# A key mask moved from TensorE products into the distances of an attention, and another order of loads in the feed-forward after it

## The chip, the cores and the metric

The kernel runs on one core of a Trainium2 chip. The metric is the time of one execution on the device in microseconds (us); the median of three runs stands for a kernel. A core has TensorE (PE: matrix products and transposes; PEld is its loading of weights, which overlaps the products), VectorE (DVE), ScalarE (ACT), GpSimd (POOL) and SyncE (SP). Each engine takes its instructions in the order in which they were written down for it and stops at one whose inputs or buffers are not ready. SyncE does no arithmetic: its queue issues nearly all transfers between the large memory (HBM) and the on-chip memory (SBUF). Products land in PSUM, from where VectorE or ScalarE must fetch them.

## The reference

Two transformer blocks run one after the other on an input of 4 batches x 1024 rows x 512 columns; each has 16 heads of 32 columns and a feed-forward of width 2048. Only the first block is touched by the change. Cut to what matters:

```
h = layer_norm(x) * (1 + scale) + shift           # scale, shift from the condition
q, k, v = split(h @ Wqkv)
scores = q @ k.T / sqrt(32) - torus_dist * torus_scale[head]
scores = where(mask[key], scores, -1e30)
x = x + softmax(scores) @ v @ Wout
x = x + gelu(layer_norm(x) @ W1 + b1) @ W2 + b2
```

`torus_dist` is one matrix of 1024 x 1024 for all batches and heads, `mask` has one bit for each batch and key, and `torus_scale` one number for each head. In the inputs of these runs every mask bit is set. The second block has an attention without mask or distances, and quantised linear layers.

## The kernel before

**Stages.** The kernel runs in four stages: first attention (to about 1590 us), first feed-forward (to about 2475), second attention (to about 3740), second feed-forward.

**The first attention** is worked off in units. A unit is a batch b, a group hg of four heads, and a tile of 128 query rows; the loops run over 4 batches, 4 head groups and 8 query tiles, 128 units in all. For each unit and each head j there is a tile `e` of 128 x 1024 values (queries x keys):

1. `begin` (L679 to L691) has GpSimd scale the distances of the query tile by the head's `torus_scale` into `e` (L689). At the first head it issues the load of that query tile's distances (L686); there are two buffers (`dp`).
2. `scores` (L258) makes, for one half c of the keys at a time, the four heads' scores (L267; the query is scaled by minus one over the root of 32, so that signs are reversed). Then, where there is a mask, four more products (L274), each of one row of ones with one row of the mask, add 1e30 at masked keys in the same PSUM bank. `masked` (L587) makes that row for a batch: it loads the bytes of the mask and GpSimd turns them into bf16 (L596).
3. `half_l0` (L694) lets VectorE add scores and `e`, write the sum back to `e`, and keep the row's running minimum (L696).
4. `weigh` lets ScalarE take the exponential (L450).
5. `turn` transposes the weights on TensorE, four blocks at a time (L291), and ScalarE or VectorE copies them to tiles `pt` (L294), whose tags pt0 and pt1 hold the two halves of the keys.
6. `product` multiplies them with v (L303), once for two units.

**Order.** All engines' orders are written out by hand: in the loop at the end of `attention` unit i makes its scores while unit i-1 is transposed and unit i-3's pair is multiplied. After each half, two `begin` calls of unit i+1 follow. Into eight slots of each unit a plan puts pieces of other work: the next head group's q, k and v (L648, L666), the last batch's output projection (`project`: loads of x at L471, products at L722, a VectorE add at L728, a store at L729), the statistics and transposed input of the next batch, and `sums`, which prepares combinations of W1 and W2 for the feed-forward and stores them as w1s and w2s. SyncE's queue holds all their transfers in the same written order.

**Buffers.** `e` tiles come from a pool of 9 (`sp`), `pt` tiles from 6 for each tag.

**The first feed-forward** works on 8 blocks of 512 rows, with seven products in place of eight at either layer (the numbered combinations 1 to 7 of quarters). `first(f)` does the first layer for one of eight pieces f of the width (L1060); its weights come with `load_w1` (L1006), one ring of two for numbers 1, 2, 6, 7, 5 (tile w1e, L1009) and one for 3, 4 (w1l, L1011). `second(n)` does the second layer for number n in the order 1, 2, 6, 7, 5, 3, 4 (L1121) and issues the loads of the next number's weights (w2q, L1025) ahead, from W2 itself or from w2s. Each `second` has two steps, 14 in a block; at some of them work for the next block is done: `rows` loads its four input tiles (L961, 1 MB), `normed` normalises them, four `turned` transpose them, `summed` makes the input's combinations. Every second step advances `beside`, which quantises the second block's weights piece by piece: `ternary` loads a piece (tile wpiece, L192, a pool `stage` of 2), reduces or scales it on VectorE and converts it on GpSimd. At its end `quantised_input` prepares the second attention's first input through tiles `xn`.

Of the kernel before, what the change touches and what calls it, by code (L numbers as in the profile page):

```python
# [30 lines left out]
F32 = mybir.dt.float32  # L31
BF16 = mybir.dt.bfloat16
U8 = mybir.dt.uint8
# [20 lines left out]
FMAX = 3.0e38  # L54
BIG = 1e30

MAGIC = 12582912.0
# [10 lines left out]

Order = namedtuple("Order", "evict exps block back even odd")
ORDER_L0 = Order(("AAAA", "AAAD"), ((1, 2), (1, 2)), 2, (1, 2), (1, 2, 3, 5, 6, 7), (3, 6))  # L70
ORDER_L1 = Order(("AADA", "AAAD"), ((1, 2), (2, 2)), 0, (0, 2), (2, 6, 7), (2, 3, 6, 7))


@with_exitstack
def two_blocks(ctx: ExitStack, tc: tile.TileContext, a: dict, out: bass.AP):
# [18 lines left out]
    nc.gpsimd.memset(ones, 1.0)  # L94
    onesb = const.tile([P, P], BF16, name="onesb")
    nc.gpsimd.memset(onesb, 1.0)
    eps_ln = const.tile([P, 1], F32, name="eps_ln")
# [85 lines left out]
    def ternary(stage, small, psum, mean, src, dst):  # L183
# [6 lines left out]
        def load(view):  # L190
            w = stage.tile([P, 2 * D], F32, name="wpiece")[:, :size]
            nc.sync.dma_start(w.rearrange("p (m n) -> p m n", m=shape[1]), view)  # L192
            return w
# [33 lines left out]

    def attention(pools, parts, softmax, clean, masked, pieces, early, guarded, order, aside, last):


# [19 lines left out]
        stats, prep, qkv, project = parts  # L250
        heads, sums, pt, es, lows, o_tiles, mask, accs = {}, {}, {}, {}, {}, {}, {}, {}

# [3 lines left out]
        def scores(u, c):  # L256
            b, hg, qc, qi = u
            qt = qc * NQ + qi  # L258
            if c == 0:
                if qi == 0:  # L260
                    sums[b, hg, qc] = small.tile([P, NQ, HPG], F32, name="sums")
                lows[u] = small.tile([P, HPG, 2], F32, name="low")
            qT, kT, _ = heads[b, hg]
            s = [ps_s.tile([P, 512], F32, name="scores", tag="s") for _ in range(HPG)]
            for j in range(HPG):
                rows = slice(j * HD, (j + 1) * HD)
                nc.tensor.matmul(  # L267
                    s[j], lhsT=qT[rows, bass.ts(qt, P)], rhs=kT[rows, bass.ts(c, 512)],
                    start=True, stop=mask[b] is None,
                )  # L270
            if mask[b] is not None:
                for j in range(HPG):
                    row1 = slice(j * HD, j * HD + 1)
                    nc.tensor.matmul(  # L274
                        s[j], lhsT=onesb[row1, :], rhs=mask[b][row1, bass.ts(c, 512)],
                        start=False, stop=True,
                    )
            for j in range(HPG):
                half(es[u, j], lows[u][:, j, :], c, s[j])
# [4 lines left out]
        def turn(u, j, h2, engine):  # L284

            b, hg, qc, qi = u
            if qi == 0:
                pt[b, hg, qc, j, h2] = pts.tile([P, LT // 2, QC], F32, name="pt", tag=f"pt{h2}")
            tr = ps_mm.tile([P, LT // 2, P], F32, name="tr", tag="mm")
            for k in range(LT // 2):  # L290
                nc.tensor.transpose(  # L291
                    tr[:, k, :], es[u, j][:, bass.ts(h2 * (LT // 2) + k, P)], ident
                )
            engine(pt[b, hg, qc, j, h2][:, :, bass.ts(qi, P)], tr)  # L294
# [106 lines left out]
        for s, n in enumerate(late):  # L401
            plan.setdefault(s, []).insert(0, (begun, n))
        mask[0] = masked(0)
        for j in range(HPG):
            start(units[0], j)
        ready = None
        with tc.manual_schedule(engines=ALL):
            for i in range(end + (3 if last else nu)):
# [3 lines left out]
                for c in range(2):  # L412
# [28 lines left out]
                    if i + 1 < end:  # L441
                        after = units[i + 1]
                        if c == 0 and after[0] not in mask:
                            mask[after[0]] = masked(after[0])
                        for j in (0, 1) if c == 0 else (2, 3):
                            start(after, j)
# [16 lines left out]
    with ExitStack() as st:  # L463
# [13 lines left out]
        dp = st.enter_context(tc.tile_pool(name="l0d", bufs=2))  # L477
        sp = st.enter_context(tc.tile_pool(name="l0s", bufs=9))
        small = st.enter_context(tc.tile_pool(name="l0small", bufs=4))
# [107 lines left out]

        def masked(b):

            if b == 0:  # L590
                m8 = m0
            else:
                m8 = tmp.tile([P, L], U8, name="m8", bufs=1)
                nc.sync.dma_start(m8, a["mask"][b].partition_broadcast(P))
            m = tmp.tile([P, L], BF16, name="maskb")
            nc.gpsimd.tensor_scalar(m, m8, -BIG, BIG, ALU.mult, ALU.add)  # L596
            return m

# [78 lines left out]

        dists, ahead = {}, [dist0]

        def begin(b, hg, qt, j):  # L680
            if j == 0:
                if ahead:
                    dists[qt] = ahead.pop()
                else:
                    dists[qt] = dp.tile([P, L], F32, name="dist")
                    nc.sync.dma_start(dists[qt], a["L0_cond_torus_dist"][0, bass.ts(qt, P), :])  # L686
            h = hg * HPG + j
            e = sp.tile([P, L], F32, name="e")
            nc.gpsimd.tensor_scalar(  # L689
                e, dists[qt], tscale[:, h : h + 1], 1.0, ALU.mult, ALU.mult  # L690
            )  # L691
            return e

# [39 lines left out]
        def sums():  # L733
# [44 lines left out]
            (small, pts, tmp, op, ps_s, ps_mm, ps_acc), (stats, prep, qkv, project),  # L778
            (begin, half_l0, exponentials), clean, masked,
            (LT + 1, LT + 2 * KT + 4, 24, 1 + 3 * LT, 12, [2] * 6), early=False, guarded=True,  # L780
# [14 lines left out]

    def modulate(pool, x, rstd, rows):
        xn = pool.tile([P, D], F32, name="xn")
        nc.vector.scalar_tensor_tensor(xn, x, rstd, rows[:, 0, :], ALU.mult, ALU.mult)  # L798
        nc.gpsimd.tensor_tensor(xn, xn, rows[:, 1, :], ALU.add)  # L799
        return xn  # L800
# [23 lines left out]
    def quantised_input(n, b, source, scale, pools, engine):  # L824


        adap, xp, tmp, small, psum, home = pools
        rows = ada_load(adap, n, b)
# [3 lines left out]
        for t in range(LT + 4):  # L832
            if t < LT:
                at = b * LT + t
                x = xp.tile([P, D], F32, name="xr")
                nc.sync.dma_start(x, source[at])
                xns[t] = modulate(tmp, x, scale[:, at : at + 1], rows)
            if 0 <= t - 2 < LT:
# [22 lines left out]
    with ExitStack() as st:  # L861
# [8 lines left out]
        tmp = st.enter_context(tc.tile_pool(name="f0t", bufs=3))  # L870
        stage = st.enter_context(tc.tile_pool(name="f0st", bufs=2))
        adap = st.enter_context(tc.tile_pool(name="f0ada", bufs=1))
# [41 lines left out]
        def beside():  # L914
# [22 lines left out]
            for n in (1, 2):  # L937
# [16 lines left out]
            yield from quantised_input(  # L954
                1, 0, x2, rms2, (adap, xin, tmp, small, ps_mm, w1p), nc.vector
            )
# [49 lines left out]
        def load_w1(f):  # L1006

            e = w1ring.tile([P, 5, 2, P], F32, name="w1e")
            nc.sync.dma_start(e, w1s[:, f, :5])  # L1009
            late = w1ring.tile([P, 2, 2, P], F32, name="w1l")  # L1010
            nc.sync.dma_start(late, w1s[:, f, 5:])  # L1011
            return {
                1: e[:, 0], 2: e[:, 1], 6: e[:, 2], 7: e[:, 3], 5: e[:, 4], 3: late[:, 0],
                4: late[:, 1],
            }

# [157 lines left out]
        with tc.manual_schedule(engines=ALL):  # L1174
            done = None
            for blk in range(nblk):
# [3 lines left out]
                if blk + 1 < nblk:  # L1180
# [14 lines left out]

                    steps[1], steps[4], steps[11] = [rows], [normed], [summed]
                    for k in range(KT):
                        steps[7 + k] = [lambda k=k: turned(k)]
                block(now["x"], now["t"], steps, blk + 1 < nblk)
# [66 lines left out]
    with ExitStack() as inner:  # L1266
# [12 lines left out]
        def first_of_ffn():  # L1279

            row_scale3(0, B - 1)
            pools = adap, xp, utmp, small, ps_mm, w1p
            yield from quantised_input(2, 0, x3, rms3, pools, nc.gpsimd)
# [4 lines left out]
        def prep(b):  # L1288
            home = hp if b % 2 else w1p
            pools = adap, xp, utmp, small, ps_mm, home  # L1290
            return quantised_input(1, b, x2, rms2, pools, nc.gpsimd) if b else iter(())
# [40 lines left out]
        def half_l1(e, low, c, s):  # L1332
# [6 lines left out]
            (small, pts, utmp, op, ps_s, ps_mm, ps_acc), (stats, prep, qkv, project),  # L1339
            (begin, half_l1, exponentials), nc.scalar.copy, lambda b: None,  # L1340
            (0, LT + 4, 12, LT + 4, 8, [1] * 4), early=True, guarded=False, order=ORDER_L1, aside=None,
# [9 lines left out]
    with ExitStack() as inner:  # L1351
# [16 lines left out]
        def normed(t):  # L1368
            xs[t] = xfp.tile([P, D], F32, name="xr")
            nc.sync.dma_start(xs[t], x3[t])  # L1370
            if t < LT:
                xqTs[t] = xqT[2, 0][:, :, bass.ts(t, P)], deqs[2, 0][:, t : t + 1]
                return
            if t % LT == 0:
                rows[t // LT] = ada_load(adap, 2, t // LT)
            xns[t] = modulate(fp, xs[t], rms3[:, t : t + 1], rows[t // LT])

# [152 lines left out]
```

## Time and profile before

| | us |
|---|---|
| median of three runs (4037.19 to 4039.2) | 4037.45 |
| the profiled execution | 4035.59 |
| its span in the profile | 4033.8 |
| first attention, 31 to 1590 | 1559 |
| first feed-forward, 1590 to 2475 | 885 |

How to read the profile: a row of a group names the line of the kernel, the engine, the operation, its output and inputs by the program's names, their shapes and the number of instructions; behind the bar stand the busy time in us and the mean length of one in ns; behind the second bar the idle time of the engine just before these instructions, and what ended it. The lengths of successive products overlap[...]; distances between starts show their price better. In a list in order of time a line holds start and length in us, and in brackets how long the engine had stood idle and what released it. The chain of waits goes from the last instruction back through whatever released each one; its shares say which lines set the end. DMA share is the mean busy share of the core's 16 DMA engines.

### The profile page before, as it was taken

What the parts mean: (1) busy time and instruction counts of PE and PEld (TensorE: products, weight loads), DVE (VectorE), ACT (ScalarE), POOL (GpSimd) and SP (SyncE); (2) the same over time, 40 slices, a digit from 0 to 9 for tenths busy, and PEclk for the clock granted to TensorE, in tenths of its full rate; (3) what the DMA queues carried; (4) which work ended last, traced back from release to release, by engine and by line L of the source; (5) the groups of instructions that cost most, each with busy time, mean ns of one, the idle gap of its engine ahead of it and who ended that gap; (6) DMA issues with size and microseconds to landing.
All of it is one profiled execution on the core that took longest, in us unless ns stands there. A gap on an engine that the chain in (4) does not pass through costs nothing.

```text
span 4033.8 us, 80643 instructions
## 1 busy us (share of the span) xinstructions
PE 3912.5 (97%) x30352; PEld 2591.5 (64%) x30403; DVE 2669.2 (66%) x6706; ACT 2557.4 (63%) x4666; POOL 1357.1 (34%) x1468
## 2 busy tenths in 40 slices
PE   8999999999999999999999999999999999999999
PEld 5666556655665565788878886666566566565554
DVE  5666565656664556555555644788788888778798
ACT  5777667766776677222222223888888788888676
POOL 3444344434443442343344430020120211202677
PEclk9999999999999999999999999999999999999999
DMA  4222222222222212666677542000100100101321
GB/s 146 69 77 78 67 89 73 81 74 89 73 80 75 78 59 93 193 221 213 210 243 230 188 150 89 1 28 4 40 27 2 43 17 12 43 2 35 136 74 45
DMA packets 198909, 357.68 MB, mean 89 GB/s; under 512 B 19108, under 2 KB 86220, under 8 KB 198392
## 3 DMA queue, kind: packets, MB, share of 16 engines
q1 hardware_dynamic: 197256, 348.77, 27.2%
q8 instruction: 240, 3.93, 0.4%
q10 hardware_dynamic: 1264, 3.75, 0.3%
q14 instruction: 149, 1.22, 0.1%
HBM read 303.13 MB, written 49.32 MB: 87 GB/s over the span
## 4 chain that ended last, share of the span: by engine, by line
PE 85%; ACT 7%; DVE 3%; DMA 2%; issue 1%; POOL 0%; SPq 0%; POOLq 0%; ACTq 0%; DVEq 0%
PE tr L291 21%; PE scores L267 13%; PE acc L303 12%; PE qk_ps L648 5%; ACT e L450 4%; PE v_ps L666 3%; PE out_ps L722 3%; ACT pt L294 3%; PE pw L1060 3%; PE pz L1060 3%; PE py L1060 3%; PE px L1121 3%; PE h_ps L1409 2%; PE o_ps L1448 2%; PE py L1121 2%; PE pw L1121 2%
## 5 line engine op out<-in xcount | busy, mean ns | idle before, releaser
L294 ACT COPY pt<-tr 128x512 f32<-128x512 f32 x1664 | 908.6, 593 | 572.6 <-PE tr L291 568.5
L291 PEld LDWEIGHTS tr<-ident,e 128*128 128x128 f32 x8192 | 897.9, 141 | 526.7 <-issue 256.9
L450 ACT ACTIVATE e<-e,low 128x1024 f32<-128x1024 f32 x1024 | 1183.8, 1164 | 2.7 <-DVE e L1333 2.0
L291 PE MATMUL tr<-ident,e 128*128 128x128 f32 x8192 | 1129.7, 279 | 35.7 <-ACT e L450 18.4
L689 POOL TENSOR_SCALAR e<-dist,tscale 128x1024 f32<-128x1024 f32 x512 | 572.2, 1121 | 910.8 <-PE tr L291 812.2
L696 DVE CUSTOM_DVE_ANT_0 e<-scores,e,low 128x512 f32<-128x512 f32 x512 | 353.9, 747 | 340.9 <-PE scores L274 340.9
L303 PE MATMUL acc<-pt,v 128*32 128x256 f32 x8192 | 498.4, 384 | 0.0
L303 PEld LDWEIGHTS acc<-pt,v 128*32 128x32 f32 x8192 | 241.4, 110 | 250.8 <-issue 119.9
L696 DVE CUSTOM_DVE_ANT_0 e<-scores,e 128x512 f32<-128x512 f32 x512 | 323.1, 687 | 113.4 <-PE scores L274 113.4
L1333 DVE TENSOR_SCALAR_CACHE_REDUCE e<-scores,low 128x512 f32<-128x512 f32 x512 | 353.6, 747 | 66.9 <-PE scores L267 66.1
L294 DVE COPY pt<-tr 128x512 f32<-128x512 f32 x384 | 264.1, 688 | 195.9 <-PE tr L291 195.9
L1333 DVE TENSOR_SCALAR_CACHE_REDUCE e<-scores 128x512 f32<-128x512 f32 x512 | 322.8, 686 | 28.8 <-PE scores L267 27.8
L267 PE MATMUL scores<-qkT 32*128 32x512 f32 x2048 | 329.3, 640 | 2.4 <-ACT qkT L1324 1.4
L267 PE MATMUL scores<-kT,qT 32*128 32x512 f32 x2048 | 317.1, 640 | 0.8 <-DVE kT L661 0.8
L1315 POOL COPY v<-qk 128x128 f32<-128x128 f32 x128 | 40.1, 314 | 661.4 <-DVE qk L1312 510.7
L648 PE MATMUL qk_ps<-hT,wqkv 128*128 128x512 f32 x512 | 255.2, 595 | 0.0
L450 ACT ACTIVATION_READ_ACCUMULATOR e<-e,low 128x1 f32 x1024 | 210.8, 206 | 0.0
L1066 ACT ACTIVATE a<-y,vcols 128x256 f32<-128x256 f32 x128 | 65.1, 508 | 196.9 <-DVE y L1082 104.5
L1074 ACT COPY s<-px 128x256 f32<-128x256 f32 x64 | 22.8, 356 | 236.0 <-PE px L1060 197.0
L267 PEld LDWEIGHTS scores<-kT,qT 32*128 32x128 f32 x2048 | 95.6, 183 | 97.7 <-issue 59.6
L799 POOL TENSOR_TENSOR xn<-xn,ada 128x512 f32<-128x512 f32 x64 | 81.5, 1274 | 193.0 <-DVE xn L798 193.0
L267 PEld LDWEIGHTS scores<-qkT 32*128 32x128 f32 x2048 | 100.4, 183 | 69.1 <-issue 31.6
(229 smaller groups left out, 5626.7 us busy)
## 6 DMA issues: line engine op xcount, KB each, us to landing
dist<-n_L_cond_torus_dist_dram SPq DMA_DIRECT2D x128, 512.0 KB
w1e<-w1s SPq DMA_DIRECT2D x64, 640.0 KB
xr<-x SPq DMA_DIRECT2D x136, 256.0 KB
w2q<-w2s SPq DMA_DIRECT2D x128, 256.0 KB
w2q<-in_L_cond_W_dram SPq DMA_DIRECT2D x96, 256.0 KB
x_in<-in_x_dram SPq DMA_DIRECT2D x84, 256.0 KB
w1l<-w1s SPq DMA_DIRECT2D x64, 256.0 KB
x<-xr SPq DMA_DIRECT2D x64, 256.0 KB
```

Source lines behind the costliest of these rows:

```text
L267: nc.tensor.matmul(s[j], lhsT=qT[rows, bass.ts(qt, P)], rhs=kT[rows, bass.ts(c, 512)], start=True, stop=mask[b] is None,)
L291: nc.tensor.transpose(tr[:, k, :], es[u, j][:, bass.ts(h2 * (LT // 2) + k, P)], ident)
L294: engine(pt[b, hg, qc, j, h2][:, :, bass.ts(qi, P)], tr)
L303: nc.tensor.matmul(acc[j * HD : (j + 1) * HD, :], lhsT=v[:, k, j * HD : (j + 1) * HD], rhs=pt[b, hg, qc, j, k // (LT // 2)][:, k % (LT // ...
L450: nc.scalar.activation(e, e, AF.Exp, bias=low, scale=-1.0, accum_out=total)
L648: nc.tensor.matmul(mm, lhsT=wqkv[:, k, bass.ds(n * D + hg * P, P)], rhs=hT[b][:, k, bass.ts(half, 512)], start=(k == 0), stop=(k == KT - 1),)
L666: nc.tensor.matmul(mm[:, i, :], lhsT=hT[b][:, k, bass.ts(half * 4 + i, P)], rhs=wqkv[:, k, bass.ds(2 * D + hg * P, P)], start=(k == 0), st ...
L689: nc.gpsimd.tensor_scalar(e, dists[qt], tscale[:, h : h + 1], 1.0, ALU.mult, ALU.mult)
L696: nc.vector.tensor_tensor_reduce(out=e, in0=s, in1=e, op0=ALU.add, op1=ALU.min, scale=1.0, scalar=low[:, 0:1] if c else 3.0e38, accum_out= ...
L1060: nc.tensor.matmul(o, lhsT=w[n][:, k, :], rhs=moving[n][:, k, :], start=k == 0, stop=k == 1)
L1121: nc.tensor.matmul(p[:, t], lhsT=hid[f][n][:, bass.ts(t, P)], rhs=w[f // 2][:, f % 2], start=f == 0, stop=f == FH - 1,)
L1333: nc.vector.tensor_scalar(e[:, bass.ts(c, 512)], s, -SCALE, low[:, 0:1] if c else 3.0e38, ALU.mult, ALU.min, accum_out=low[:, c : c + 1],)
```

## The change

The mask products and `masked` are gone, and with them the row of ones. In their place the distances are marked: for each batch GpSimd makes the 16-bit pattern of a bf16 NaN at masked keys and zero elsewhere (`make_bar`), and VectorE adds it to each of the batch's eight distance tiles (`bar`), which are stored in HBM (`barred`) while they are used for the first head group. Head groups 1 to 3 load the stored tiles. GpSimd's scaling now takes the minimum with 1e30 as its second operation, where it multiplied by 1 before; [...]masked keys get 1e30.

The load of a distance tile is now issued one unit earlier in the written order, in the first `begin` of the unit before; the next batch's mask is loaded at the last head group's first tile and converted at its fourth. The `bar` of a tile stands behind the last `begin` of the unit before it. The pool of `e` has 10 buffers, pt0 of the first attention 5.

In the first feed-forward w1 is loaded in three tiles (numbers 1, 2; then 6, 7, 5; then 3, 4); the pieces of `ternary` have three buffers, which `quantised_input` shares for its `xn`; and `rows`, `normed`, `turned` and `summed` stand one step later. The core of the diff:

```diff
-ORDER_L0 = Order(("AAAA", "AAAD"), ((1, 2), (1, 2)), 2, (1, 2), (1, 2, 3, 5, 6, 7), (3, 6))
+ORDER_L0 = Order(("AAAA", "AAAD"), ((1, 2), (1, 2)), 2, (1, 2), (1, 2, 3, 5, 6, 7), (3, 6), (5, 6), ((0, 1), (2, 3)))
...
-                    start=True, stop=mask[b] is None,
+                    start=True, stop=True,
                 )
-            if mask[b] is not None:
-                for j in range(HPG):
-                    row1 = slice(j * HD, j * HD + 1)
-                    nc.tensor.matmul(
-                        s[j], lhsT=onesb[row1, :], rhs=mask[b][row1, bass.ts(c, 512)],
-                        start=False, stop=True,
-                    )
...
-                pt[b, hg, qc, j, h2] = pts.tile([P, LT // 2, QC], F32, name="pt", tag=f"pt{h2}")
+                pt[b, hg, qc, j, h2] = pts.tile([P, LT // 2, QC], F32, name="pt", tag=f"pt{h2}", bufs=order.pts[h2])
...
-        sp = st.enter_context(tc.tile_pool(name="l0s", bufs=9))
+        sp = st.enter_context(tc.tile_pool(name="l0s", bufs=10))
...
+        def load_mask(b):
+            m8s[b] = tmp.tile([P, L], U8, name="m8", bufs=1)
+            nc.sync.dma_start(m8s[b], a["mask"][b].partition_broadcast(P))
+
+        def make_bar(b):
+            bits = tmp.tile([P, L], mybir.dt.uint16, name="bar", bufs=1)
+            nc.gpsimd.tensor_scalar(bits, m8s.pop(b), -QNAN, QNAN, ALU.mult, ALU.add)
+            bars[b] = bits[:, :].bitcast(BF16)
+
+        def load_dist(b, hg, qt):
+            d = dists[b, hg, qt] = dp.tile([P, L], F32, name="dist")
+            nc.sync.dma_start(
+                d, barred[b][qt] if hg else a["L0_cond_torus_dist"][0, bass.ts(qt, P), :]
+            )
+
+        def bar(b, qt):
+            d = dists[b, 0, qt]
+            nc.vector.tensor_tensor(d, d, bars[b], ALU.add)
+            nc.sync.dma_start(barred[b][qt], d)
+
+        make_bar(0)
+        bar(0, 0)
...
         def begin(b, hg, qt, j):
-            if j == 0:
-                if ahead:
-                    dists[qt] = ahead.pop()
-                else:
-                    dists[qt] = dp.tile([P, L], F32, name="dist")
-                    nc.sync.dma_start(dists[qt], a["L0_cond_torus_dist"][0, bass.ts(qt, P), :])
+            n = (b * NHG + hg) * LT + qt + 1
+            after = n // (NHG * LT), n // LT % NHG, n % LT
+            if after[0] == B:
+                after = None
...
-                e, dists[qt], tscale[:, h : h + 1], 1.0, ALU.mult, ALU.mult
+                e, dists[b, hg, qt], tscale[:, h : h + 1], BIG, ALU.mult, ALU.min
             )
+            if j == 0 and after:
+                load_dist(*after)
+                if hg == NHG - 1 and b + 1 < B and qt == 0:
+                    load_mask(b + 1)
+            if j == HPG - 1:
+                dists.pop((b, hg, qt))
+                if hg == NHG - 1 and b + 1 < B and qt == 3:
+                    make_bar(b + 1)
+                if after and after[1] == 0:
+                    bar(after[0], after[2])
             return e
...
-        stage = st.enter_context(tc.tile_pool(name="f0st", bufs=2))
+        stage = st.enter_context(tc.tile_pool(name="f0st", bufs=3))
...
-            e = w1ring.tile([P, 5, 2, P], F32, name="w1e")
-            nc.sync.dma_start(e, w1s[:, f, :5])
-            late = w1ring.tile([P, 2, 2, P], F32, name="w1l")
-            nc.sync.dma_start(late, w1s[:, f, 5:])
+            w = {}
+            for at, numbers in ((0, (1, 2)), (2, (6, 7, 5)), (5, (3, 4))):
+                n = len(numbers)
+                t = w1ring.tile([P, n, 2, P], F32, name=f"w1_{at}")
+                nc.sync.dma_start(t, w1s[:, f, at : at + n])
+                w |= {number: t[:, i] for i, number in enumerate(numbers)}
+            return w
...
-                    steps[1], steps[4], steps[11] = [rows], [normed], [summed]
+                    steps[2], steps[5], steps[12] = [rows], [normed], [summed]
                     for k in range(KT):
-                        steps[7 + k] = [lambda k=k: turned(k)]
+                        steps[8 + k] = [lambda k=k: turned(k)]
```

## The prediction

> **What bounds the kernel now.** I read the totals first, then the stages, the chain of waits of the first attention, the groups, and short stretches in order of time. The totals, and busy time by stage (span, PE, PEld, DVE, ACT, POOL; then TensorE clock, DMA share, GB/s):
>
> ```profile
> PE 3912.5 (97%) x30352; PEld 2591.5 (64%) x30403; DVE 2669.2 (66%) x6706; ACT 2557.4 (63%) x4666; POOL 1357.1 (34%) x1468
> ```
> ```profile
> 31.00:1590.00 1559.00, 1545.81 (x13199) 944.82 (x13198) 912.43 (x2630) 1120.28 (x2031) 627.43 (x639) 1.00 0.24 74
> 1590.00:2475.00 885.00, 854.47 (x3995) 722.69 (x3994) 466.05 (x763) 178.64 (x370) 325.04 (x378) 0.99 0.64 205
> ```
>
> The first attention (31 to 1590 us) keeps TensorE busy 99% of its time, with ScalarE at 72%, VectorE at 59%, GpSimd at 40% and the DMA engines at 24%. The first feed-forward (1590 to 2475) has TensorE at 97% and DMA at 64%. Only these two stages are touched. The chain of waits of the first 1600 us, by line, and the groups of the touched instructions:
>
> ```profile
> by line: PE tr L291 30.0%; PE scores L267 17.3%; PE acc L303 14.7%; PE qk_ps L648 13.2%; PE v_ps L666 7.0%; PE out_ps L722 5.5%; PE scores L274 3.8%; ACT e L450 1.8%; ACT pt L294 1.6%; PE acc L325 0.8%; PE tr_x L456 0.7%; issue 0.6%; PE tr_
> ```
> ```profile
> L689 POOL TENSOR_SCALAR e<-dist,tscale 128x1024 f32<-128x1024 f32 x512 | 572.2, 1121 | 910.8 <-PE tr L291 812.2 <-ACT e L450 29.6 <-issue 28.4
> ...
> L696 DVE CUSTOM_DVE_ANT_0 e<-scores,e 128x512 f32<-128x512 f32 x512 | 323.1, 687 | 113.4 <-PE scores L274 113.4
> ...
> L1121 PE MATMUL py<-w2q,a 128*128 128x256 f32 x512 | 124.3, 395 | 20.7 <-DMA w2q<-w2s 11.5 <-DMA w2q<-in_L_cond_W_dram 9.1
> ...
> L274 PE MATMUL scores<-maskb,onesb 1*128 1x512 bf16 x1024 | 120.1, 376 | 0.0
> ```
>
> The mask products (L274) stand on the chain with 3.8% of 1600 us, 61 us; ScalarE's two lines together have 3.4%. VectorE waits for L274, never the other way round for long. GpSimd's scalings wait for free buffers, not the reverse.
>
> **Part 1, the mask products go.** There are 1024, in 256 groups of four (128 units, two halves). Their busy time of 120.1 us overlaps with neighbours, so I take distances between starts. A half of the first attention, and one of the second attention, which has no mask:
>
> ```profile
> 717.73 1.14 PE L267 MATMUL scores<-kT,qT 32*128 32x512 f32 x8
> 718.69 0.40 PE L274 MATMUL scores<-maskb,onesb 1*128 1x512 bf16 x4
> 719.02 1.09 PE L291 MATMUL tr<-ident,e 128*128 128x128 f32 x8
> ```
> ```profile
> 2707.08 1.14 PE L267 MATMUL scores<-qkT 32*128 32x512 f32 x8
> 2708.15 0.66 PE L291 MATMUL tr<-ident,e 128*128 128x128 f32 x4
> ```
>
> With masks, scores to the next transpose is 1.29 us; the masks themselves take 719.02 - 718.69 = 0.33 us. Counted so, the saving is 256 x 0.33 = 84 us. But the Trainium skill, TensorEngine Tiling (Array Packing), Key Properties, says that a change of tiling mode drains TensorE: scores and masks both use 32-row tiles, the transposes the full array, so the drain before the transposes stays. The second attention agrees: without masks the same distance is 1.07 us, so a group is worth 1.29 - 1.07 = 0.22 us: **256 x 0.22 = 56 us**. I take that; the chain's 61 us (0.24 each) is the upper end. Lower end: half, 28 us, if ScalarE sets the pace in the short units. Why I don't expect that: in a bare pair of units (7.6 + 10.9 = 18.5 us from score start to score start, at 404) ScalarE has 8 exponentials at 1.14 and 14 copies at 0.47, 15.7 us, still under 18.5 - 0.86 = 17.6.
>
> **Part 2, GpSimd's scaling with a minimum.** No row has a minimum on GpSimd. Nearest is the same instruction with two multiplies, 1121 ns; a multiply and an add on 2048 elements (L1427) takes 1972, the same 0.83 ns per further element, so the second operation's kind does not show. I take 1.12 us again: nothing. Upper end: the price of its two-input add (L799, 1274 ns per 512, so 2.5 us): 10.0 us per unit, over the bare pairs alone (20.0 against 17.6): 19 such pairs, up to +46 us. No gain is possible, as GpSimd isn't on the chain.
>
> **Part 3, the barred distances.** New: 32 VectorE adds of 128x1024, 32 stores and no more loads than now (128); four conversions of a mask, as now (L596, 1.04 us). VectorE takes 424 ns for 256 columns (L1082) and 692 for 512 (L1086), so I estimate 1.23 us for 1024; 32 x 1.23 = 39 us of an engine that is 41% idle. They stand at the end of a unit, before the evictions of the next, where VectorE looks like this (a bare unit):
>
> ```profile
> 403.83 0.69 DVE L294 COPY pt<-tr 128x512 f32<-128x512 f32 x1 [1.22 <-PE tr L291]
> 405.14 0.69 DVE L696 CUSTOM_DVE_ANT_0 e<-scores,e 128x512 f32<-128x512 f32 x1 [0.62 <-PE scores L274]
> ```
>
> Free time there is 0.62 us (0.3 less once the masks are gone), so an add delays the four evictions by about 0.9 us. That reaches TensorE only where the second scores follow 3 us later and wait for a bank; the units of a first head group measure 7.6, 10.9, 16.2, 14.8, 19.0, 14.0, 24.3, 15.6 us in batches 1 to 3. So one or two adds per batch are on the path: about 4 x 0.9, **+4 us**. Ends: 0, and all 32 exposed, +39.
>
> A rule speaks against this part. SBUF — State Buffer, Who interferes with whom: a VectorE instruction with two SBUF inputs and a GpSimd one that reads SBUF block each other; whichever starts first holds the pair to its end. The trace agrees:
>
> ```profile
> 1724.91 0.68 DVE L998 TENSOR_TENSOR t<-hT,hT 128x512 f32<-128x512 f32 x1
> 1725.08 1.20 POOL L222 TENSOR_SCALAR wq<-wpiece 128x768 bf16<-128x768 f32 x1 [2.56 <-DVE wpiece L216]
> 1725.63 1.19 DVE L999 TENSOR_TENSOR hT<-hT 128x512 f32<-128x512 f32 x1
> ```
>
> The GpSimd op takes 1.20 in place of 0.83, the second add 1.19 in place of 0.69. By the rule every add could wait out one scaling, 32 x 1.12 = +36 us more. I don't charge it: the scalings of the unit after next wait for this very add, and those of the next unit end in the middle of the current one, so GpSimd is mostly idle at that moment.
>
> DMA: 32 stores of 512 KB, 16.8 MB. At 24% busy they are hidden; without that cover, at the 306 GB/s of the first 31 us, 1.7 us each, 55 us. SyncE's queue: a store waits for its add at the end of a unit; behind it stand the loads of x (L471), the stores of x1 (L729), the quarters (L744) and the next distance (L686). The next distance has at least half a unit to land (4 us or more); x loads in that part already wait for L728 and the store before them (134.5 us in SyncE's waits), so they lose little. At the start the first add runs behind the normalisation that ends at 25.5, and GpSimd's four scalings then end near 32, before the first eviction at 33.28: 0.
>
> One pt buffer less (5 of the first half's tiles) is neutral: when the fifth is needed for the second transposed pair, the four products that free the oldest have just run ahead of it on TensorE. The tenth e buffer lets GpSimd run a quarter of a unit earlier, which nobody waits for: 0.
>
> **Part 4, the first feed-forward.** TensorE idles 20.7 us for w2q (row L1121 above) and 3.0 us for w1e (row L1060 px). One case:
>
> ```profile
> 1810.21 0.33 SPq L192 DMA_DIRECT2D wpiece<-in_L_cond_w_ada_dram  x1
> 1810.64 0.38 SPq L1025 DMA_DIRECT2D w2q<-w2s  x1
> ...
> 1814.44 1.13 PE L1121 MATMUL py<-w2q,a 128*128 128x256 f32 x4 [1.16 <-DMA w2q<-w2s]
> ```
>
> SyncE stands at L192 until a weight piece is released by work that VectorE does behind the normalisation; the w2 load behind it lands late. A third piece buffer lets L192 pass one step earlier: of the 11.5 us I take 8. The other 9.1 are loads issued late, then in company of 1 MB of x1 (L961); that megabyte moves one step later: 3 gained, but it now stands ahead of half the loads for the third product: 7 blocks x 0.5 = 3.5 lost. w1 in three loads (64 more issues, 0.4 us each on SyncE, which has room) starts the needed 256 KB alone: 2 gained. The input sums end near 1731 in place of 1728, before TensorE's 1733 to 1735: 0. Sum **-9 us**; ends -24 (all idle time) and +15 (7 blocks with a stall of about 2).
>
> **Sum** against the profiled execution (4035.6 us, span 4033.8 and 1.8 around it): 4035.6 - 56 + 4 - 9 = 3974.6. The median of the runs shown stands 1.9 above it, so **3977** (3976.5 rounded up).
>
> **Rivals.** (a) ScalarE takes over as the bound: for it speaks that ScalarE is already at 72% of a stage that gets shorter, with 54 us (3.4%) on the chain; against it the 15.7 of 17.6 above. Masks 28: 4035.6 - 28 + 4 - 9 + 1.9 = 4004. (b) The feed-forward's new order of loads collides at 205 GB/s: -56 + 4 + 15 gives 4001. (c) Slower: the add waits on VectorE for its own distance, whose load was issued only half a unit before (256 KB issued at 1810.64 served TensorE at 1814.44, 3.8 us); in-order VectorE holds the evictions, TensorE the banks. At 3 us each, 32 x 3 = 96: 4035.6 - 56 - 9 + 96 + 1.9 = 4068. It decides from (56 + 9)/32 = 2.0 us each on the path; against it, the units there are mostly 14 to 24 us long. (d) No change, if mask products were hidden: their 61 us on the chain says no.
>
> **How the numbers follow.** Likeliest 0.66, (a) 0.15, (b) 0.12, (c) 0.05, (d) 0.02. About 0.2% (8 us) can be told from no change. Low end: -61 - 24 and bars free: 4035.6 - 85 + 1.9 = 3952. High end 4006 takes in (a) and (b). Faster 0.92 (a little of (a) and (b) falls short), same 0.03, slower 0.05.
>
> **What would show it.** No L274; scores to transposes 1.07 us; the scaling still 1.12; 32 adds near 1.23 with little of TensorE's wait behind them; bare pairs near 17.6; L1121's idle under 12; the stages near 1508 and 876 us. Wrong if the scaling exceeds 2 us, if VectorE waits for distances, or if ScalarE's lines grow past 80 us on the chain.

## The result

The changed kernel takes 4486.2 us (median of 4, 4480.3 to 4489.1) against 4037.3 us before (median of 4): 1.111 times the time, 95% interval 1.109 to 1.113. The forecast was 3977 us, faster. Totals and the first attention's stretch of the changed kernel (it now ends near 2045 us; columns as before: span, PE, PEld, DVE, ACT, POOL, then TensorE clock, DMA share, GB/s), and the chain of waits up to there:

```profile
PE 4152.2 (93%) x29379; PEld 2684.9 (60%) x29379; DVE 2729.0 (61%) x6738; ACT 2565.9 (57%) x4666; POOL 2687.4 (60%) x1467
```
```profile
31.00:2045.00 2014.00, 1782.74 (x12097) 1036.06 (x12096) 973.07 (x2650) 1120.13 (x2014) 1956.41 (x642) 0.89 0.20 65
```
```profile
by line: POOL e L696 27.7%; PE tr L284 18.5%; PE scores L267 12.5%; PE acc L296 9.8%; PE qk_ps L658 7.3%; issue 6.4%; PE out_ps L739 3.4%; PE v_ps L676 3.2%; DVE e L713 2.5%; ACT e L440 2.2%; ACT pt L287 1.6%; DMA x_in<-in_x_dram 0.7%; PE a
```

GpSimd was busy for 40% of this stage and is now busy for 1956 of 2014 us. It stands first on a chain on which it did not stand at all. The groups of the touched instructions say why:

```profile
L696 POOL TENSOR_SCALAR e<-dist,tscale 128x1024 f32<-128x1024 f32 x512 | 1900.1, 3711 | 48.1 <-DVE mv L520 1.6
L713 DVE CUSTOM_DVE_ANT_0 e<-scores,e 128x512 f32<-128x512 f32 x512 | 339.7, 689 | 587.5 <-POOL e L696 508.3
L267 PE MATMUL scores<-kT,qT 32*128 32x512 f32 x2048 | 485.4, 674 | 210.5 <-DVE low L713 209.6
...
L603 DVE TENSOR_TENSOR dist<-dist,bar 128x1024 f32<-128x1024 f32 x32 | 42.8, 1339 | 5.0 <-DMA dist<-n_L_cond_torus_dist_dram 5.0
L1138 PE MATMUL py<-w2q,a 128*128 128x256 f32 x512 | 117.3, 381 | 9.4 <-DMA w2q<-w2s 6.0 <-DMA w2q<-in_L_cond_W_dram 3.3
```

One scaling with the minimum takes 3.71 us, where one with two multiplies took 1.12. Four make 14.8 us per unit, more than a unit lasted (12.2 us on average). VectorE waits 508 us for them and holds the score banks, and TensorE, which idled 0.8 us before its scores in the kernel before, idles 210 us behind it. Most of the rest of the longer stage counts as busy TensorE time: scores that start two at a time as banks fall free (485 us busy for 317), and work at a lower clock (0.89 for 1.00). The last two rows are those of the prediction's other steps: 32 adds of 1.3 us whose own waits come to 5 us, and a wait for w2q that fell in this row from 20.7 to 9.4 us (in all rows of the line from 20.8 to 12.4).

### The profile page after: what moved, and what is told of

Read it like the earlier page. It is cut to its first block, busy times and chain, and to the rows that moved or that the text cites. A ratio compares the mean times of both kernels' runs of the same rounds, so it can differ in the third digit from the quotient of the medians.

```text
span 4478.5 us, 78517 instructions
## 1 busy us (share of the span) xinstructions
PE 4152.2 (93%) x29379; PEld 2684.9 (60%) x29379; DVE 2729.0 (61%) x6738; ACT 2565.9 (57%) x4666; POOL 2687.4 (60%) x1467
## 3 DMA queue, kind: packets, MB, share of 16 engines
q14 instruction: 149, 1.22, 0.1%
## 4 chain that ended last, share of the span: by engine, by line
PE 70%; POOL 13%; ACT 7%; DVE 4%; issue 4%; DMA 2%; SPq 0%; POOLq 0%; ACTq 0%; DVEq 0%
PE tr L284 17%; POOL e L696 13%; PE scores L267 11%; PE acc L296 10%; ACT e L440 4%; PE qk_ps L658 3%; ACT pt L287 3%; PE pw L1077 2%; PE pz L1077 2%; PE py L1077 2%; PE px L1138 2%; PE h_ps L1426 2%; PE out_ps L739 2%; PE o_ps L1465 2%; PE py L1138 2%
## 5 line engine op out<-in xcount | busy, mean ns | idle before, releaser
L696 POOL TENSOR_SCALAR e<-dist,tscale 128x1024 f32<-128x1024 f32 x512 | 1900.1, 3711 | 48.1 <-DVE mv L520 1.6
L284 PEld LDWEIGHTS tr<-ident,e 128*128 128x128 f32 x8192 | 958.3, 148 | 600.9 <-issue 325.5
L284 PE MATMUL tr<-ident,e 128*128 128x128 f32 x8192 | 1198.0, 291 | 33.7 <-ACT e L440 16.2
L713 DVE CUSTOM_DVE_ANT_0 e<-scores,e 128x512 f32<-128x512 f32 x512 | 339.7, 689 | 587.5 <-POOL e L696 508.3
L267 PE MATMUL scores<-kT,qT 32*128 32x512 f32 x2048 | 485.4, 674 | 210.5 <-DVE low L713 209.6
L296 PE MATMUL acc<-pt,v 128*32 128x256 f32 x8192 | 536.4, 406 | 0.2 <-DVE o L322 0.2
L296 PEld LDWEIGHTS acc<-pt,v 128*32 128x32 f32 x8192 | 252.4, 116 | 278.4 <-issue 159.5
L267 PEld LDWEIGHTS scores<-kT,qT 32*128 32x128 f32 x2048 | 131.6, 191 | 405.5 <-DVE low L713 325.6
L658 PE MATMUL qk_ps<-hT,wqkv 128*128 128x512 f32 x512 | 265.8, 617 | 0.0
L1110 POOL TENSOR_TENSOR a<-z,a 128x256 f32<-128x256 f32 x64 | 47.5, 741 | 279.4 <-ACT z L1083 279.4
```

The lines of the kernel that those rows point to most:

```text
L267: nc.tensor.matmul(s[j], lhsT=qT[rows, bass.ts(qt, P)], rhs=kT[rows, bass.ts(c, 512)], start=True, stop=True,)
L284: nc.tensor.transpose(tr[:, k, :], es[u, j][:, bass.ts(h2 * (LT // 2) + k, P)], ident)
L296: nc.tensor.matmul(acc[j * HD : (j + 1) * HD, :], lhsT=v[:, k, j * HD : (j + 1) * HD], rhs=pt[b, hg, qc, j, k // (LT // 2)][:, k % (LT // ...
L658: nc.tensor.matmul(mm, lhsT=wqkv[:, k, bass.ds(n * D + hg * P, P)], rhs=hT[b][:, k, bass.ts(half, 512)], start=(k == 0), stop=(k == KT - 1),)
L696: nc.gpsimd.tensor_scalar(e, dists[b, hg, qt], tscale[:, h : h + 1], BIG, ALU.mult, ALU.min)
L713: nc.vector.tensor_tensor_reduce(out=e, in0=s, in1=e, op0=ALU.add, op1=ALU.min, scale=1.0, scalar=low[:, 0:1] if c else 3.0e38, accum_out= ...
```

## The experiments

Where the stages stand in the runs, from the first starts of their products in each trace: the first attention's scores from first to last, and from the feed-forward's first product to the second attention's first scores. These two columns are of one execution each; two executions of the same version (multiply by one) gave 1497.5 and 1493.6 us of scores, and the four runs with the old feed-forward 838.8 to 847.9 us for it. Each ratio is to runs of the kernel before on the same chip.

| | scores, us | feed-forward, us | median of the runs, us | to before (95%) |
|---|---|---|---|---|
| before | 1547.0 | 843.0 | 4037.3 | |
| changed | 2013.6 | 821.9 | 4486.2 | 1.111 (1.109 to 1.113) |
| multiply by one | 1497.5 | 824.1 | 3969.6 | 0.983 (0.982 to 0.985) |
| the same, old feed-forward | 1496.6 | 838.8 | 3980.9 | 0.986 (0.985 to 0.987) |
| before, new feed-forward | 1546.9 | 828.3 | 4026.5 | 0.998 (0.997 to 0.999) |
| before, no mask products | 1491.3 | 847.9 | 3982.2 | 0.987 (0.985 to 0.988) |
| before, with the minimum | 2021.1 | 839.6 | 4509.8 (one run) | |

**The minimum taken back.** The first run keeps the whole change but for that one operation. So that masked keys still come out, 1e30 is added to their distances in place of a NaN (right for positive scales, which these inputs have). No key is masked in these inputs, so no run shows either mark at work, nor what GpSimd's minimum makes of a NaN.

```diff
-                e, dists[b, hg, qt], tscale[:, h : h + 1], BIG, ALU.mult, ALU.min
+                e, dists[b, hg, qt], tscale[:, h : h + 1], 1.0, ALU.mult, ALU.mult
...
-            bits = tmp.tile([P, L], mybir.dt.uint16, name="bar", bufs=1)
-            nc.gpsimd.tensor_scalar(bits, m8s.pop(b), -QNAN, QNAN, ALU.mult, ALU.add)
-            bars[b] = bits[:, :].bitcast(BF16)
+            bars[b] = tmp.tile([P, L], BF16, name="bar", bufs=1)
+            nc.gpsimd.tensor_scalar(bars[b], m8s.pop(b), -BIG, BIG, ALU.mult, ALU.add)
```

> The changed kernel, with GpSimd's second operation a multiply by one again instead of the minimum with 1e30; masked keys get 1e30 added to the distance in place of NaN, which comes to the same for positive scales. Theory (the minimum alone makes the kernel slower, since one scaling takes 3.7 us for 1.12, four of them 14.8 us per unit): the scaling is back at 1.12 us and the time is the forecast of the rest, 3977 us (3960 to 3995). Rival 1 (the stores, adds and waits of the barred distances cost a good part of it): above 4060 us. Rival 2 (the lower TensorE clock, 0.89 in the first stage for 1.00, is a cause of its own and comes from the denser products): the clock of the first stage stays under 0.95 and the time above 4060 us.

Measured: 3969.6 us, 0.983 of before. Its stage and its rows:

```profile
31.00:1530.00 1499.00, 1482.19 (x12101) 908.08 (x12100) 945.95 (x2650) 1108.74 (x2012) 628.23 (x639) 1.00 0.27 88
```
```profile
L695 POOL TENSOR_SCALAR e<-dist,tscale 128x1024 f32<-128x1024 f32 x512 | 572.3, 1125 | 857.6 <-PE tr L284 441.6 <-ACT e L440 201.6 <-ACT pt L287 122.2
...
L602 DVE TENSOR_TENSOR dist<-dist,bar 128x1024 f32<-128x1024 f32 x32 | 39.0, 1219 | 3.8 <-DMA dist<-n_L_cond_torus_dist_dram 3.8
...
L592 POOL TENSOR_SCALAR bar<-m 128x1024 bf16<-128x1024 uint8 x4 | 4.3, 1081 | 20.1 <-DMA m<-in_mask_dram 19.8
```

The scaling is back at 1.12 us, GpSimd at 628 us, the clock at 1.00. Both rivals fall: stores, adds and waits are all still there, and the clock recovers with the wait. No version measured is clearly faster than this one. Measured again, beside later runs, it gave 3971.2 us, 0.984 (0.982 to 0.985):

> The run with the multiply by one once more, to stand beside the next two on the same chip: 3970 us, 0.983 of the kernel before; scores of the first attention from first to last in about 1497 us.

**The minimum put into the kernel before.** The converse, with the mask products kept:

```diff
-                e, dists[qt], tscale[:, h : h + 1], 1.0, ALU.mult, ALU.mult
+                e, dists[qt], tscale[:, h : h + 1], BIG, ALU.mult, ALU.min
```

> The kernel before, mask products and all, with one word changed: GpSimd's second operation is the minimum with 1e30. Theory: GpSimd bounds the first attention, 512 x 3.7 = 1900 us and some 100 us of its other work, so that the stage ends near 2040 us as in the changed kernel and the time is 4470 to 4500 us; the mask products are hidden. Rival 1 (the barred distances cost a good part): clearly below, 4250 or so.

Measured in one run: 4509.8 us, scores in 2021 us, as long as in the changed kernel. The single operation makes the whole loss of the stage, and hides the mask products: with GpSimd as the bound their removal is worth 7.5 us (2021.1 against 2013.6) where it is worth 55.7 without the minimum.

**The operations by themselves.** None of the kernel's work is done here; six instructions in a row of each form, GpSimd unless VectorE is named:

```diff
+    for _ in range(N):
+        g.tensor_scalar(new(), x, s, 1.0, ALU.mult, ALU.mult)
+    for _ in range(N):
+        g.tensor_scalar(new(), x, s, BIG, ALU.mult, ALU.min)
+    for _ in range(N):
+        g.tensor_scalar(new(), x, s, -BIG, ALU.mult, ALU.max)
+    for _ in range(N):
+        g.tensor_scalar(new(), x, s, 1.0, ALU.mult, ALU.add)
+    for _ in range(N):
+        g.tensor_scalar(new(), x, BIG, 1.0, ALU.min, ALU.mult)
...
+        v.tensor_scalar(new(), x, s, BIG, ALU.mult, ALU.min)        # L112
```

> No part of the reference is computed: six instructions in a row of each of several forms on GpSimd, 128x1024 in fp32 where no width is said, then two forms on VectorE. Theory (the minimum itself is slow on GpSimd): multiply+multiply and multiply+add 1.1 us, multiply+minimum 3.7 us, minimum+multiply slow as well; at 512 and 256 columns 1.9 and about 1.0 us if the price is by element. Rival (something else of the stage slows the scaling, such as VectorE on a shared port, or the large constant): multiply+minimum alone near 1.1 us here. If only a minimum is slow, multiply+maximum is near 1.1 us; if every comparison is, 3.7 us. VectorE's multiply+minimum under 1 us.

The groups of that run (the diff's instructions are L92, L94, L96, L98, L100 and L112 in order; L102 and L104 are L94's form on 512 and 256 columns, L106 a two-input add):

```profile
L94 POOL TENSOR_SCALAR e<-d,ts 128x1024 f32<-128x1024 f32 x6 | 22.2, 3700 | 0.5
L96 POOL TENSOR_SCALAR e<-d,ts 128x1024 f32<-128x1024 f32 x6 | 22.2, 3700 | 0.5
L100 POOL TENSOR_SCALAR e<-d 128x1024 f32<-128x1024 f32 x6 | 21.8, 3626 | 0.5
...
L106 POOL TENSOR_TENSOR e<-d 128x1024 f32<-128x1024 f32 x6 | 13.8, 2337 | 0.1
L102 POOL TENSOR_SCALAR e<-d,ts 128x512 f32<-128x512 f32 x6 | 12.0, 1994 | 0.5
L104 POOL TENSOR_SCALAR e<-d,ts 128x256 f32<-128x256 f32 x6 | 6.8, 1138 | 0.5
L98 POOL TENSOR_SCALAR e<-d,ts 128x1024 f32<-128x1024 f32 x6 | 6.6, 1118 | 0.1
L92 POOL TENSOR_SCALAR e<-d,ts 128x1024 f32<-128x1024 f32 x6 | 6.6, 1118 | 6.1 <-DMA ts<-_L_cond_torus_scale_dram 6.1
...
L112 DVE TENSOR_SCALAR e<-d,ts 128x1024 f32<-128x1024 f32 x6 | 4.1, 749 | 0.0
```

Multiply with add costs exactly what multiply with multiply does, 1.118 us. A minimum or a maximum, second or first, costs 3.63 to 3.70 us with nothing else running: the stage around it plays no part. The sign of the constant plays none either, and its size does not explain the price: the row L592 above, with -1e30 as factor and 1e30 as addend, takes 1.08 us. A comparison with a small constant was not run. From 512 to 1024 columns it is (3700 - 1994)/512 = 3.3 ns per column, four times the 0.83 of the fast forms. A minimum is even dearer than a two-input add (2.34 us), which the prediction had taken for the upper end. VectorE does the same in 0.75 us.

**How many minima the stage bears.** The fast version with the minimum for some of the four heads of each unit:

```diff
-                e, dists[b, hg, qt], tscale[:, h : h + 1], 1.0, ALU.mult, ALU.mult
+                e, dists[b, hg, qt], tscale[:, h : h + 1], *(
+                    (BIG, ALU.mult, ALU.min) if j < 2 else (1.0, ALU.mult, ALU.mult)
+                )
```

> The same with the minimum for one head of four: 3.71 + 3 x 1.12 = 7.1 us per unit, under every unit's length. Theory: within 8 us of the run with the multiply by one. If each minimum costs its surplus wherever it stands: a quarter of the loss, some 125 us.

> The run with the multiply by one, with the minimum for two of the four heads of each unit. GpSimd then needs 2 x 3.71 + 2 x 1.12 = 9.7 us per unit, less than the mean unit of some 11.7 us, more than half a bare pair (8.8 us). Theory (time is lost only where GpSimd's four scalings exceed the unit): 0 to 33 us above the run with the multiply by one. If each minimum costs its surplus wherever it stands, half of the loss of the changed kernel: some 250 us.

> The minimum for three heads of four: GpSimd needs 3 x 3.70 + 1.12 = 12.2 us per unit and about 0.6 for its other work, more than the mean unit of 11.7 us. Theory (GpSimd bounds the stage once its scalings exceed the unit): 128 x 12.8 = 1640 us for the scores in place of 1497, so some 120 to 150 us above the run with the multiply by one, near 4100 us. If the loss were in proportion to the number of minima, three quarters of 515, 4355 us.

| heads with a minimum | GpSimd's scalings per unit, us | scores, us | median, us | to before (95%) |
|---|---|---|---|---|
| 0 | 4.5 | 1497.5 | 3969.6 | 0.983 (0.982 to 0.985) |
| 1 | 7.1 | 1510.1 | 3983.8 | 0.987 (0.986 to 0.989) |
| 2 | 9.6 | 1508.4 | 3982.6 | 0.987 (0.985 to 0.989) |
| 3 | 12.2 | 1723.0 | 4198.7 | 1.040 (1.039 to 1.041) |
| 4 (changed kernel) | 14.8 | 2013.6 | 4486.2 | 1.111 (1.109 to 1.113) |

The loss is not in proportion to the minima. Two cost hardly anything, three cost 226 us of scores and four 516. The three-head run was forecast too low (1640 for 1723). I had compared GpSimd's need with the mean unit. One can take the 127 unit lengths of the fast version one by one instead and put GpSimd's need wherever that is longer:

| heads with a minimum | need per unit, us | longer by this reckoning, us | measured, us |
|---|---|---|---|
| 2 | 9.6 | 35 | 11 |
| 3 | 12.2 | 160 | 226 |
| 4 | 14.8 | 430 | 516 |

With the 0.4 us of GpSimd's other work per unit (56 us in 128 units) it is 197 and 477 for three and four. So the reckoning is not the whole account: with two heads most short units cost nothing, since GpSimd can be some tiles ahead; with three and four more is lost than the unit lengths tell. What makes the rest is open; the clock below may have a share in it.

The 13 us with one head were not expected either: 7.1 us lie under every unit. Unit by unit, all are as long as in the fast version, within 0.3 us, except those of the last head groups of batches 0 to 2, where VectorE normalises the next batch's input (L634). VectorE in the fast version and with one minimum, in order of time:

```profile
1077.57 2.48 DVE L634 TENSOR_SCALAR x_in<-x_in,mv,rstd 128x512 f32<-128x512 f32 x4
```
```profile
1087.38 5.03 DVE L634 TENSOR_SCALAR x_in<-x_in,mv,rstd 128x512 f32<-128x512 f32 x4
1092.33 0.74 DVE L714 CUSTOM_DVE_ANT_0 e<-scores,e,low 128x512 f32<-128x512 f32 x1
```
GpSimd at that time, with one minimum:
```profile
1083.45 12.47 POOL L695 TENSOR_SCALAR e<-dist,tscale 128x1024 f32<-128x1024 f32 x6 [3.72 <-ACT e L440]
```

The four normalisations take 5.03 us for 2.48 while GpSimd's scalings run without a gap, and the evictions wait behind them. It is not the length of a minimum that they wait for. In the changed kernel four of them stand inside one minimum and take 2.20 us:

```profile
413.43 3.70 POOL L696 TENSOR_SCALAR e<-dist,tscale 128x1024 f32<-128x1024 f32 x1
413.99 2.20 DVE L635 TENSOR_SCALAR x_in<-x_in,mv,rstd 128x512 f32<-128x512 f32 x4
```

What holds a normalisation up is the start of a scaling of either kind (see the last section). In the fast version one start falls just before the four. With one minimum GpSimd is later there, and four scalings, three multiplies and a minimum, start one behind the other, 0.11 to 0.23 us before each of the four, which take 1.26 to 1.34 us. To see whether the surplus comes from these units, the minimum was left out in the last head groups:

```diff
+                    (BIG, ALU.mult, ALU.min) if j < 1 and hg < NHG - 1 else (1.0, ALU.mult, ALU.mult)
```

> The minimum for one head of four, but in the first three head groups alone. With one head of four in all groups the scores took 12.6 us longer than without a minimum, all of it in the units of the last head group where VectorE normalises the next batch's input; the normalisation's median was 1.26 us for 0.68. Theory (VectorE's normalisation and a GpSimd scaling hold each other up, and a scaling of 3.7 us holds longer): the surplus is gone, scores in 1497 us and the time within 4 us of the run with the multiply by one. Rival (the surplus is spread over all minima): three quarters of it stay, some 9 us.

Measured: 3969.0 us, 0.983 (0.982 to 0.985); scores in 1494.8 us beside 1493.6 in the repeat of the fast version; the normalisation's median is 0.64 us in both. The surplus came from those units alone, and was not spread over the minima. The forecast came true, but its reason, that a longer scaling holds VectorE longer, is not what the traces show. For two heads the surplus is about as large, but there the normalisation's median is 0.54 us, and VectorE waits 12 us for scalings and 6 us for x. Of its 11 us, 3.6 stand in the short units at the end of the stage (7.4 and 10.0 us); the cause of the rest is open.

**The parts that were forecast as small.** The mask products left out of the kernel before (no mask is applied there, though its row is still made), the attention's part alone and the feed-forward's part alone:

```diff
-            if mask[b] is not None:
-                for j in range(HPG):
-                    row1 = slice(j * HD, j * HD + 1)
-                    nc.tensor.matmul(
-                        s[j], lhsT=onesb[row1, :], rhs=mask[b][row1, bass.ts(c, 512)],
-                        start=False, stop=True,
-                    )
```

> The kernel before with the mask products left out and nothing in their place: the mask isn't applied, which these inputs, whose masks are all ones, can't show. It prices the products alone: by distances between starts 56 us, 3981 us; by the chain's share 61 us, 3976; by the bare length of the products 84 us, 3953; if ScalarE sets the pace instead, 28 us, 4009. Its difference to the run with the attention's part is the price of the adds and stores, forecast at 4 us.

The scores take 1491.3 us for 1547.0: 55.7 us, 0.22 us for each of 256 groups. The distance between starts was right: from scores to the next transposes it is 1.29 us before and 1.07 here, each the median of 256 halves. The 0.33 us of the products themselves were not all to be had.

```diff
-        stage = st.enter_context(tc.tile_pool(name="f0st", bufs=3))
+        stage = st.enter_context(tc.tile_pool(name="f0st", bufs=2))
...
-                    steps[2], steps[5], steps[12] = [rows], [normed], [summed]
+                    steps[1], steps[4], steps[11] = [rows], [normed], [summed]
...
```

> As the run with the multiply by one, with the first feed-forward as in the kernel before (w1 in two loads, two piece buffers, the old steps). By the sum of the prediction: 4037 - 56 + 4 = 3985 us. If the feed-forward's part gives nothing it equals the run with that part; if that part costs time, it is faster than it.

The scores take 1496.6 us, 5.3 us more than in the run without mask products (4 forecast for adds, stores and the other order of loads). Unit by unit, 0.9 us of it stand where the adds were expected to show, in the second units of the first head groups of batches 1 to 3, and 4.4 us in the last head groups of batches 0 to 2, where VectorE normalises the next batch's input. The two executions of the fast version differ by 4.1 us in one such head group alone, so the 5.3 is not firm. In total time the two can't be told apart (3980.9 and 3982.2).

```diff
-        stage = st.enter_context(tc.tile_pool(name="f0st", bufs=2))
+        stage = st.enter_context(tc.tile_pool(name="f0st", bufs=3))
...
-                    steps[1], steps[4], steps[11] = [rows], [normed], [summed]
+                    steps[2], steps[5], steps[12] = [rows], [normed], [summed]
...
```

> The kernel before with the feed-forward's part of the change alone. By the prediction -9 us: 4028 us, with TensorE's wait for w2q under 12 us where it was 20.7; ends 4013 (all idle time gone) and 4052 (the new order of loads collides).

```profile
L1121 PE MATMUL py<-w2q,a 128*128 128x256 f32 x512 | 121.8, 392 | 10.6 <-DMA w2q<-w2s 5.2 <-DMA w2q<-in_L_cond_W_dram 5.2
L1060 PE MATMUL px<-hT,w 128*128 128x256 f32 x256 | 66.9, 383 | 0.0
```

Measured: 4026.5 us, 9.5 below the 4036.1 of the same chip (6 to 13 by the interval). TensorE waits 10.6 us for w2q in this row, 14.3 in all rows of the line (20.8 before), and nothing for w1 (3.0 before): 9.5 us of waits less. (The stage's column, of one execution each, falls by 14.7.) Which of its three edits gave how much wasn't tried.

## Why the prediction was wrong

**Part 2 failed, and it alone makes the loss.** "the same 0.83 ns per further element, so the second operation's kind does not show. I take 1.12 us again: nothing." The rows behind it showed multiplies and an add, none a comparison, so they could not speak for a minimum, and my upper end of 2.5 us came from a two-input add, which is no comparison either. Measured is 3.70 us, and at that price GpSimd needs 14.8 us of units of 11.7: 516 us of scores against the fast version. The prediction did say that it would be wrong if the scaling exceeded 2 us: the place was named, the price not.

**The bound's consequence was also too small.** Part 2 valued 2.5 us as a matter of the bare pairs alone, up to 46 us from 19 pairs. The sum itself was too large: the fast version has 14 pairs of units under 20.0 us, and 10.0 us per unit would lengthen them by 23 us together. The two-head run (9.6 us per unit, 13 us lost) lies within both; from there the loss rises steeply, which the prediction had nothing for.

**Part 1 held**: 55.7 us for 56, and by the distance on which it rested: scores to transposes is 1.08 us in this stretch of the changed kernel (707.90 to 708.98), 1.07 forecast. That a drain makes up what remains, as the cited page has it, no run isolates.

```profile
707.90 1.14 PE L267 MATMUL scores<-kT,qT 32*128 32x512 f32 x8
708.98 1.09 PE L284 MATMUL tr<-ident,e 128*128 128x128 f32 x8
```

**Part 3 held for the add itself, and only in part for its cost.** An add takes 1.22 us (1.23 estimated). But of the 5.3 us for 4, only 0.9 lie where Part 3 had placed its 4; that the sums agree is luck. The lock between VectorE and GpSimd, which I did not charge to the adds, cost them next to nothing for the reason given: in the fast version no scaling ran beside 31 of the 32. It showed at the normalisations instead, which I had not looked at because they are not part of the change.

**Part 4 held**: 9.5 us for 9.

**The rivals.** (a) did not come: without the minimum TensorE is busy 1482 of 1499 us. (b) did not come. (c) had the right sign by the wrong mechanism: in the changed kernel VectorE's adds wait 5 us in all for distances, and its evictions 508 us for GpSimd. Without the minimum the whole sum, 3977, stands against 3969.6 measured.

## What to carry to other kernels

A group's row prices an operation, not an engine: if the changed instruction has another arithmetic operation, a row with the same shape and engine says nothing until that operation is in it, and the range has to carry that. Ask first how often the instruction runs and how much the engine could bear per unit of the loop (here 11.7/4 = 2.9 us), for that tells whether the unknown decides the result. A comparison that GpSimd would do hundreds of times is better avoided by the choice of the constant: 1e30 in the distances needed no minimum, as long as the scales are positive.

## What the runs showed of the hardware

- GpSimd's scalar instruction with a minimum or maximum takes 3.3 times as long as with a multiply or an add (3.70 for 1.12 us on 128x1024 in fp32), whether the comparison stands first or second.
- A GpSimd scaling of 128x1024 holds VectorE's adds and normalisations back for about 0.9 us from its start, whether it lasts 1.12 or 3.70 us. Two adds of the changed kernel, each behind the minimum that was running:

```profile
35.51 3.70 POOL L696 TENSOR_SCALAR e<-dist,tscale 128x1024 f32<-128x1024 f32 x1
35.65 2.05 DVE L603 TENSOR_TENSOR dist<-dist,bar 128x1024 f32<-128x1024 f32 x1 [1.93 <-DMA dist<-n_L_cond_torus_dist_dram]
```
```profile
43.09 3.70 POOL L696 TENSOR_SCALAR e<-dist,tscale 128x1024 f32<-128x1024 f32 x1
44.59 1.22 DVE L603 TENSOR_TENSOR dist<-dist,bar 128x1024 f32<-128x1024 f32 x1
```

  An undisturbed add takes 1.22 us. The first began 0.14 us behind a minimum and waited until 0.97 us after that one's start (0.14 + 2.05 - 1.22). The second began 1.50 us behind one and lost nothing, though the minimum ran on. Neither did, within 0.01 us, any of the 35 adds in the runs with three and four minima that began at least 1 us behind a minimum and before its end. SBUF — State Buffer, Who interferes with whom, in the Trainium skill, says that of VectorE in a two-port mode and GpSimd the one that issues first has the shared ports for the whole instruction, and the prediction took the same for an add with two inputs. For a minimum that is too strong: held to its end at 417.13, the four normalisations shown above could not have been done at 416.19. In which mode they ran the trace does not show.
- TensorE's granted clock fell where it had to wait: 0.89 over the first attention of the changed kernel, 0.90 in the kernel before with the minimum, 1.00 without the minimum in either. After a wait of 2.67 us, a stretch with full work ran at 0.50, and eight transposes took 1.97 us in place of 1.09:

```profile
729.17 1.60 PE L267 MATMUL scores<-kT,qT 32*128 32x512 f32 x2 [2.67 <-DVE low L713]
730.71 1.97 PE L284 MATMUL tr<-ident,e 128*128 128x128 f32 x8
```
```profile
731.00:735.00 4.00, 4.00 (x14) 2.86 (x13) 0.81 (x4) 2.31 (x4) 3.91 (x2) 0.50 0.37 107
```

The lower clock follows the loss rather than makes it, since GpSimd is busy 97% of the stage and the clock is back at 1.00 when the minimum goes. What it adds of its own was not separated.
